# A two-layer graph network on one core: attention of the second layer moved from a stage of its own into the edge loop before it

## The chip, the core and the metric

The kernel runs on one core of a Trainium2 chip. The core has five engines with instruction streams of their own: TensorE (PE; its weight loads are shown apart, as PEld), VectorE (DVE), ScalarE (ACT), GpSimd (POOL) and SyncE (SP), and 16 DMA engines between the memory outside (DRAM here) and the core's own. Each engine takes its instructions in program order and waits at an instruction for what it needs; a transfer is issued by SP, ACT or POOL and then runs by itself. The metric is the device time of one execution in microseconds.

## The reference: what is computed

There are 12500 nodes with 256 features and 200000 directed edges (`src`, `dst`), sorted by `dst`. In short:

```python
h = relu(layernorm(x))
h = h @ W_pre + b_pre
for W, b in ((W1, b1), (W2, b2)):            # two graph convolutions
    z = h @ W
    h = relu(segment_sum(z[src] * norm, dst) + b)   # a self loop at each node as well
x = x + h @ W_post + b_post
h = relu(layernorm(x))
xt = (h @ weight).reshape(n, 4, 64)          # attention
alpha = softmax(leaky_relu((xt[src] * attn_l).sum(-1) + (xt[dst] * attn_r).sum(-1)), over the 4 heads)
out = x + (sum over heads of alpha[i] * xt[dst[i]], repeated 4 times)   # i < 12500: node i uses edge i
```

`norm` is 1/sqrt(degree of source) times 1/sqrt(degree of target). What matters later is the last step: row i of the output uses edge number i, so only the first 12500 edges take part. Edges are sorted by target, so the targets of these edges lie in the first nodes, while their sources lie anywhere.

## The kernel before

**Tiles.** Nodes are cut into 98 tiles of 128 (called windows, `w`). Edges are cut into 112 chunks of 14 tiles of 128 edges (`J = 14`, `CE = 1792`); the last chunk has 9. The 1792 edges of a chunk have targets within 128 nodes of the chunk's first one, so that the whole chunk is summed in one accumulator.

**Preparation.** Up to about 130 us the kernel loads x and the edges, counts the degrees and writes the normed rows to a table in DRAM.

**The edge loop** is `convolve` (from L1185), used twice: pass 1 (first convolution) and pass 2 (second). For each tile of 128 edges:
- POOL gathers 128 source rows from a table in DRAM into the buffer `fgot` (L1397, an indirect DMA). A row of the tables `parts1` and `parts2` is three bf16 parts whose sum is the fp32 row, 1.5 KB in pass 2.
- VectorE has made the chunk's one-hots `fhot` (L1243) in one instruction for all 14 tiles: for each edge a row of 128 zeros and a one at its target's place.
- TensorE adds one-hot times gathered rows to the accumulator `facc`, once for each of the three parts (L1407).

When a chunk is done, `close` copies the accumulator out (`fsums`, ScalarE), turns it (`fturn`, TensorE) and adds it into a sliding buffer of turned sums (`buf`, VectorE, at an offset read from a register). When the buffer's first 128 nodes are complete, `finish` lets a window through: in pass 1 the product with the first layer's folded weights, the split into parts and the write to `parts2`; in pass 2 (`finish2`) two products (`fpz`, `fpo`), the new x (kept in DRAM as `kept_x`), a layer norm, a turn (`fpt`) and the product with the attention weights (`fpx`, L1597).

**The order of work** is written out by hand: each step of a window is put on a list with a due tile (`at`), and after each tile's instructions the loop emits the steps that are due (`run`). The last windows, behind the last tile, run their steps one after the other.

**Buffers.** In pass 2 the gathers have four buffers of 9 tiles, so POOL can be up to 36 tiles ahead of TensorE. A buffer is free again when all its products are done.

**Attention** is a stage of its own behind pass 2 (L1640 to L1792), except for small preparations in pass 2 (`set_up`; target rows of the first chunk). Window by window `fpx` gives the products with the weights and their left and right scores; the left scores of all nodes go to the tables `table_l` and `table_e` in DRAM, the first nine windows' rows to `table_r`. The stage then handles 14 groups of 7 tiles: target rows by products with one-hots (`fends`, L1741), left scores by 98 gathers of 16 bytes a row (`fal`, L1751; those of the last three windows by products, `lacks`, for the first 14 tiles), then a softmax over four heads and the weighted sum on VectorE (`near`, `far`, `some`, `more`, `fmix`), and the output rows (`fres`).

Behind all that stands `general_path`, which runs only where a test of the edges fails (`bad_row`); here it doesn't run.

Of the kernel before, what the change touches and what calls it, by code (L numbers as in the profile page):

```python
# [10 lines left out]
I32 = mybir.dt.int32  # L11
# [402 lines left out]
def fast_path(  # L414
# [51 lines left out]
    complete = [min(max((M * c - LAG) // P, 0), NT) for c in range(NCH)] + [NT]  # L466
    assert NCH <= P and complete[NCH - 1] >= NT - 2
# [11 lines left out]
    assert AC * J == NT and AC * CE <= E and XW < NT  # L479
    table_r = dram.tile([XW * P, DR], F32, name="table_r")  # L480
    table_l = dram.tile([NT * P, H], F32, name="table_l")

    LW = 3
    table_e = dram.tile([NT * P, H], F32, name="table_e")
# [18 lines left out]
    base_b = const.tile([P, NCH], F32, name="base_b")  # L503
    row_i = const.tile([P, AC], I32, name="row_i")
# [88 lines left out]
    with tc.tile_pool(name="fprep", bufs=1) as prep:  # L593
# [233 lines left out]
        with tc.tile_pool(name="fpsum", bufs=2, space=PSUM) as psum, \  # L827
# [227 lines left out]
            wide = prep.tile([NCH, P], F32, name="wide")  # L1055
            nc.vector.tensor_copy(wide, base.to_broadcast([NCH, P]))
# [7 lines left out]
            nc.tensor.matmul(fk[:, 2, :NCH], wide, ident[:NCH, :NCH], start=True, stop=True)  # L1064
# [7 lines left out]
            for f in after:  # L1072
                f()
            after = [raw_block(ends, m, psum.tile([P, 4 * P], F32, name="ft"), j0)
                     for j0 in (8, 12)]
            nc.vector.tensor_copy(base_b, fk[:, 2, :NCH])
            nc.vector.tensor_scalar(row_i, base_b[:, :AC], lane, float(XW * P - 1), op0=ALU.add,
                                    op1=ALU.min)
# [16 lines left out]
    def check_chunks(work, psum):  # L1095

        last = E - (NCH - 1) * CE
        far = work.tile([P, 2, NCH], F32, name="far2", bufs=1)
        nc.vector.tensor_reduce(far[:, 0, :], to_t, AX.X, ALU.min)
        c, (n, r) = NCH - 1, divmod(last, P)  # L1100
        nc.vector.tensor_reduce(far[:, 1, :c], to_t[:, :c, :], AX.X, ALU.max)
        nc.vector.tensor_reduce(far[:, 1, c:], to_t[:, c, None, :n], AX.X, ALU.max)
        if r:
            nc.vector.tensor_tensor(far[:r, 1, c:], far[:r, 1, c:], to_t[:r, c, n:n + 1], ALU.max)
        pt = psum.tile([P, KC + 2, P], F32, name="fpt", bufs=1)
        for i in range(2):
            nc.tensor.transpose(pt[:NCH, i, :], far[:, i, :], ident)
        ends = work.tile([NCH, 2], F32, name="far_ends", bufs=1)
        nc.vector.tensor_reduce(ends[:, 0:1], pt[:NCH, 0, :], AX.X, ALU.min)
        nc.vector.tensor_reduce(ends[:, 1:2], pt[:NCH, 1, :], AX.X, ALU.max)  # L1110
        nc.vector.tensor_scalar(ends[:, 0:1], ends[:, 0:1], 0.0, None, op0=ALU.is_ge)
        nc.vector.tensor_tensor(ends[:, 1:2], ends[:, 1:2], keeps[:, 1:2], ALU.is_lt)
        nc.vector.tensor_mul(ends[:, 0:1], ends[:, 0:1], ends[:, 1:2])
        nc.vector.tensor_mul(ends[:, 0:1], ends[:, 0:1], keeps[:, 0:1])
        nc.tensor.transpose(pt[:1, 2, :NCH], ends[:, 0:1], ident[:NCH, :NCH])
        kept = work.tile([1, 1], F32, name="n_kept", bufs=1)
        nc.vector.tensor_reduce(kept, pt[:1, 2, :NCH], AX.X, ALU.add)
        nc.vector.tensor_add(kept, kept, counted)
        nc.vector.tensor_scalar(bad_row, kept, -1.0, float(NCH + 1), op0=ALU.mult, op1=ALU.add)
# [12 lines left out]
    def load_late(pool):  # L1132

        nc.scalar.dma_start(roots, root_t)
        for t, w in ((wb, w2), (wo, w_post), (wg[:, :, :D], w_gat)):
            nc.scalar.dma_start(t, w.rearrange("(k p) n -> p k n", p=P))
        nc.scalar.dma_start(b2c, b2.rearrange("(k p) -> p k", p=P))
        nc.scalar.dma_start(bob, b_post.partition_broadcast(P))
        attn = []
        for a in (attn_r, attn_l):  # L1140
            ar = pool.tile([P, D], F32, name="far", bufs=2)
            nc.scalar.dma_start(ar, a.rearrange("h c -> (h c)").partition_broadcast(P))
            attn.append(ar)
        return attn

    def late_weights(pool, attn):

        for i, ar in enumerate(attn):
            for k in range(KC):
                prod = pool.tile([P, H, C], F32, name="fprod", bufs=1)  # L1150
                nc.vector.tensor_mul(prod.rearrange("p h c -> p (h c)"), wg[:, k, :D], ar)
                nc.vector.tensor_reduce(wg[:, k, D + i * H:D + (i + 1) * H], prod, AX.X,
                                        ALU.add)

    def convolve(ep, table, stride, width, ahead, with_sum, psum, prepare, finish, parts, since,
                 lacking=False, raw=(), rows_p=None, behind=None):
# [28 lines left out]
        def run(now=None):  # L1185

            while due:
# [3 lines left out]
                do(d)  # L1191

# [41 lines left out]
        const_p = psum.tile([P, P if with_sum else P + D], F32, name="iota_p", bufs=1)  # L1234
        iota_p = const_p[:, :P]
        nc.vector.tensor_copy(iota_p, iota_w)
        if not with_sum:
            state["bias"] = const_p[:, P:]
            nc.vector.tensor_copy(state["bias"], bob)

# [13 lines left out]

        def hot_of(c):

            n = nj[c]
            h = new_hot(c)
            one_hots(h[:, :n, :], to_0 if lacking and c == 0 else to_t[:, c, :n])
            return h  # L1260

        def new_rows_of():
            if with_sum:
                return new_got()
            return rows_p.tile([P, ONE, 3 * stride], BF16, name="fgot", bufs=ahead)

        def late_sums():
# [3 lines left out]
            froms = new_rows_of().rearrange("p j d -> p (j d)")[:, :J * D]  # L1271
            froms = froms.rearrange("p (j d) -> p j d", d=D)
            assert stride == TW * P and D == TW * P
            for i in range(TW):
                one_hots(froms[:, :, i * P:(i + 1) * P], from_0[:, i, :])
            px = psum.tile([P, KC, P], F32, name="fpt", bufs=1)
# [100 lines left out]
        for t, (c, j) in enumerate(tiles):  # L1377
# [4 lines left out]
            if many == 1:  # L1382
                if j == 0:
                    gots = (raw + [spare])[c] if raw and c <= len(raw) else new_rows_of()
                got = gots[:, j, :]
            else:
                i = (t - since * J) % ONE
                if i == 0:
                    gots = new_rows_of()
                    if since:  # L1390
                        gots = gots.rearrange("p j d -> p (j d)").bitcast(BF16)
                        gots = gots[:, :ONE * 3 * stride].rearrange("p (j d) -> p j d", j=ONE)
                got = gots[:, i, :]
# [10 lines left out]
            if j == (5 if some else 2) and c + 1 < NCH:  # L1404
                hots[c + 1] = hot_of(c + 1)
            for i in range(many):
                nc.tensor.matmul(acc, hots[c][:, j, :], got[:, i * stride:i * stride + width],  # L1407
# [10 lines left out]
            if behind:  # L1418
                behind(t)
            run(t)  # L1420
        run()
# [51 lines left out]
    def split_rows(pool, psum):  # L1473
        rows = {}

        def load(w):
            rows[w] = pool.tile([P, D1], F32, name="frow", bufs=4)
            nc.sync.dma_start(rows[w], table1[w * P:(w + 1) * P, :])

        def step(t):  # L1480
# [3 lines left out]
            if k < NT:  # L1484
                load(k)
            if k >= 2:
                p = psum.tile([P, 4, P], F32, name="fpt", bufs=1)
                p = p.rearrange("p a b -> p (a b)")[:, :D1]
                b = pool.tile([P, 3, D1], BF16, name="frow_p", bufs=3)
# [3 lines left out]
                to_parts(p, b, parts1, k - 2)  # L1493

# [5 lines left out]
    assert 3 * D1 * ONE <= 2 * D1 * J and J * D <= 3 * D * ONE  # L1500

    with tc.tile_pool(name="psum1", bufs=1, space=PSUM) as psum, \
# [5 lines left out]
                 lambda w, b, s, pre, _: finish1(work, psum, w, b, s, pre), parts1, SINCE,  # L1508
                 raw=raw, rows_p=late, behind=split_rows(late, psum))
    ring.close()  # L1510

    ap = ctx.enter_context(tc.tile_pool(name="fatt", bufs=2))
    rows = [ap.tile([P, DR], F32, name="rows", bufs=AC) for c in range(AC)]
    EARLY = 2

    FROM = 40
    assert J % G == 0 and FROM > XW + 2 and FROM + J < NT - LW
    lates = {w: ap.tile([P, DA], F32, name="fxl", bufs=LW) for w in range(NT - LW, NT)}
    early = [ap.tile([P, G, DR], F32, name="fxe", bufs=J // G) for g in range(J // G)]
    hot_l = [ap.tile([P, CE], F32, name="hot_l", bufs=LW) for i in range(LW)]  # L1520

    def prepare2(work, w):
# [6 lines left out]
        nc.sync.dma_start(xb[:n, :], x[w * P:w * P + n, :])  # L1531
        return rb, xb

    def finish2(work, psum, w, buf, pre, bias):
        v = {"root": pre[0], "x": pre[1]}

        def d():
            pz = in_psum(psum, w, "fpz", [P, D], "facc", [P, D], 2)
# [16 lines left out]
        def f():  # L1555
            po = v["po"] = in_psum(psum, w, "fpo", [P, D], "facc", [P, D], 2)
# [4 lines left out]
        def g():  # L1561
# [9 lines left out]
            nc.scalar.activation(v["sc"], mv[:, 1:2], AF.Sqrt, bias=eps)  # L1571

# [8 lines left out]
        def i():  # L1581
            pt = v["pt2"] = in_psum(psum, w, "fpt", [P, KC, P], "fturn", [P, 2 * KC, P])
            for k in range(KC):
                nc.tensor.transpose(pt[:, k, :], v["h"][:, k * P:(k + 1) * P], ident)  # L1584

        def k():
            v["ht"] = work.tile([P, KC, P], F32, name="ht2")
            nc.scalar.activation(v["ht"], v["pt2"][:, :KC, :], AF.Copy)  # L1588
# [4 lines left out]
        def q():  # L1593
            px = in_psum(psum, w, "fpx", [P, DA], "iota_p", [P, P + D])
            px = v["px"] = px[:, d0:] if w + 1 < NT else px[:, :H]
# [4 lines left out]
        def r():  # L1600
            if w < NT - LW:
                xa = work.tile([P, DA], F32, name="fxa")
            else:
                xa = lates[w]
            nc.scalar.activation(xa[:, d0:], v["px"], AF.Copy)
            nc.scalar.dma_start(table_l[w * P:(w + 1) * P, :], xa[:, DR:])
            if w < NT - LW:
                nc.scalar.dma_start(table_e[w * P:(w + 1) * P, :], xa[:, DR:])
# [233 lines left out]
```

## Time and profile before

| what | us |
|---|---|
| median of 10 runs (4148.69 to 4157.59) | 4150.46 |
| the profiled execution | 4150.89 |
| its span, first to last instruction | 4149.1 |
| first gather of pass 1 / of pass 2 (start) | 133.9 / 2029.6 |
| last gather of pass 2 (end) | 3987.2 |
| first gather of the attention stage (start) | 4004.1 |
| POOL busy / TensorE / VectorE / ScalarE | 3107.2 / 2794.0 / 1386.7 / 620.4 |
| mean granted TensorE clock | 0.73 |

How to read the views: a *group* line gives a line of the kernel, the engine, the operation, output and inputs, shapes and count; then busy time in us and the mean of one instruction in ns; then the engine's idle time just before these instructions and what ended it. "Issue" is a gap in which the engine waited for nothing that the profile shows. Products overlap, so a group's busy time over its count is what one costs in a row of them, and less than the mean of one. A *window* line gives, for a stretch of time, the busy time of PE, PEld, DVE, ACT and POOL (with instructions), then the granted TensorE clock (1.00 is full), the mean busy share of the DMA engines and GB/s. The *chain* follows the work that ended last back to its causes; printed in order of time it gives start, length and what.

### The profile page before, as it was taken

The numbers are of one execution on the slowest core, as the hardware profiler recorded it, in microseconds if no ns is written. First come the engines' busy times: TensorE is split into PE (matmuls) and PEld (weight loads), VectorE is DVE, ScalarE is ACT, GpSimd is POOL, SyncE is SP. The second block draws the span as 40 slices with busy tenths as digits, with TensorE's granted clock in tenths as the row PEclk, the third lists the DMA queues.
The fourth block names the chain that finished last, engine by engine and source line by source line (L and its number), as shares of the span: only waits on it lengthen the run. The fifth ranks groups of instructions, "written<-read, shape, count | busy, mean of one in ns | idle before, by whom it ended". The sixth has DMA issues, their size and how long they took to land. (4 is left out here: it accounts for less than half of the span.)

```text
span 4149.1 us, 38956 instructions
## 1 busy us (share of the span) xinstructions
PE 2794.0 (67%) x13306; PEld 1909.3 (46%) x13306; DVE 1386.7 (33%) x3009; ACT 620.4 (15%) x1625; POOL 3107.2 (75%) x3299
## 2 busy tenths in 40 slices
PE   7687776767777766777666666666666666666674
PEld 5465444444444444444444444444454444444452
DVE  7677532222222222222322222222222222222238
ACT  5433210100010001001001111111111111111122
POOL 7677777777777777777777777777777777777766
PEclk7697876666666666666678877777777777777777
DMA  8688766666666666666667766776676666666766
GB/s 269 191 247 239 219 176 183 187 183 183 183 185 181 182 186 184 181 183 187 185 182 203 186 180 179 180 185 178 180 180 186 180 180 181 181 180 180 185 195 196
DMA packets 413533, 787.28 MB, mean 190 GB/s; under 512 B 101005, under 2 KB 267172, under 8 KB 413324
## 3 DMA queue, kind: packets, MB, share of 16 engines
q0 software_dynamic: 197264, 594.53, 54.3%
q1 hardware_dynamic: 170214, 173.89, 13.1%
q10 hardware_dynamic: 45846, 16.27, 1.6%
q8 instruction: 107, 1.75, 0.2%
q14 instruction: 102, 0.84, 0.1%
HBM read 692.31 MB, written 92.05 MB: 189 GB/s over the span
## 5 line engine op out<-in xcount | busy, mean ns | idle before, releaser
L1397 POOL DMA_INDIRECT fgot<-parts,fsrc_t x2720 | 2574.4, 946 | 828.6 <-issue 797.2
L1407 PE MATMUL facc<-fgot,fhot 128*128 128x256 bf16 (+2 forms) x8986 | 1943.5, 357 | 1162.6 <-DMA fgot<-parts,fsrc_t 1078.6
L1407 PEld LDWEIGHTS <-fhot 128*128 128x128 bf16 x8202 | 982.0, 121 | 1741.5 <-issue 1475.9
L1243 DVE TENSOR_TENSOR fhot<-iota_p,to_t 128x1792 bf16<-128x1792 f32 (+1 forms) x224 | 449.1, 2005 | 0.0
L1397 POOL DMA_INDIRECT fgot<-ftable,fsrc_t x336 | 318.5, 948 | 115.0 <-issue 103.3
L1468 DVE TENSOR_TENSOR fpo<-fpo,fparts 128x256 f32<-128x256 f32 x97 | 41.8, 431 | 921.5 <-ACT fo L1454 921.5
L1549 DVE SCALAR_TENSOR_TENSOR fy<-rb,fb2c,fpz 128x128 f32<-128x128 f32 x194 | 58.8, 345 | 681.5 <-PE fpz L1542 681.5
L1305 DVE TENSOR_TENSOR buf<-buf,fturn 128x256 f32 x224 | 94.5, 422 | 414.0 <-PE fturn L1208 368.4
L1407 PEld LDWEIGHTS facc<-fgot,fhot 128*128 128x128 f32 x784 | 164.7, 227 | 128.3 <-DMA fgot<-ftable,fsrc_t 79.3
L1563 DVE SCALAR_TENSOR_TENSOR fx<-fpo,fdinv,fxb 128x256 f32<-128x256 f32 x97 | 46.9, 484 | 525.1 <-PE fpo L1558 525.1
L1288 ACT ACTIVATE fsums<-facc 128x257 f32<-128x257 f32 (+1 forms) x224 | 85.4, 381 | 883.4 <-PE facc L1407 877.8
L1445 PE MATMUL fpo<-wf,buf 128*128 128x256 f32 x388 | 164.3, 571 | 25.3 <-DVE buf L1305 25.3
L1542 PE MATMUL fpz<-buf,fwb 128*128 128x128 f32 x776 | 170.8, 395 | 1.4 <-DVE buf L1305 1.4
L1542 PEld LDWEIGHTS fpz<-buf,fwb 128*128 128x128 f32 x776 | 165.0, 313 | 7.7 <-DVE buf L1305 2.0
L1450 ACT ACTIVATE fpo<-fpo,fdinv 128x256 f32<-128x256 f32 x97 | 43.1, 445 | 584.1 <-PE fpo L1446 584.1
L1445 PEld LDWEIGHTS fpo<-wf,buf 128*128 128x128 f32 x388 | 106.4, 299 | 49.3 <-DVE buf L1305 29.5
L1208 PE MATMUL fturn<-fident,self 128*128 128x128 f32 x396 | 97.2, 336 | 26.9 <-DMA self<-ftable 25.2
L1208 PE MATMUL fturn<-fident,fsums 128*128 128x128 f32 x448 | 108.9, 334 | 1.9 <-ACT frow_p L1492 1.5
L1558 PE MATMUL fpo<-fwo,fz 128*128 128x256 f32 x388 | 107.4, 402 | 0.8 <-ACT fz L1552 0.8
L1588 ACT ACTIVATE ht<-fpt 128x256 f32<-128x256 f32 x97 | 37.1, 383 | 441.3 <-PE fpt L1584 440.4
L1751 POOL DMA_INDIRECT fal<-table_l,fsrc_t x84 | 81.2, 967 | 25.6 <-issue 23.2
L1552 ACT ACTIVATE fz<-fy 128x256 f32<-128x256 f32 x98 | 40.8, 417 | 392.7 <-DVE fy L1549 344.6
(284 smaller groups left out, 2411.1 us busy)
## 6 DMA issues: line engine op xcount, KB each, us to landing
fgot<-parts,fsrc_t POOLq DMA_INDIRECT x2720
parts<-frow_p SPq DMA_DIRECT2D x98, 195.0 KB
parts<-fparts SPq DMA_DIRECT2D x98, 192.0 KB
frow<-ftable SPq DMA_DIRECT2D x98, 130.0 KB
self<-ftable SPq DMA_DIRECT2D x99, 128.0 KB
self<-ftable SPq DMA_DIRECT2D x97, 130.0 KB
ftable<-fo ACTq DMA_DIRECT2D x98, 128.0 KB
kept_x<-fx SPq DMA_DIRECT2D x98, 128.0 KB
```

The source lines that it names most:

```text
L1208: nc.tensor.transpose(v["pt"][:, i * KC + k, :], rows[:, k * P:(k + 1) * P], ident)
L1243: nc.vector.tensor_tensor(h, iota_p[:, None, :].to_broadcast([P, n, P]), to[:, :, None].to_broadcast([P, n, P]), ALU.is_equal)
L1288: nc.scalar.activation(sb, acc, AF.Copy)
L1305: nc.vector.tensor_add(b, b, v["pt"][:, :KC, :])
L1397: nc.gpsimd.indirect_dma_start(out=got, out_offset=None, in_=rows_of[:(NT - TW) * P, :] if some else rows_of[:], in_offset=bass.IndirectOf ...
L1407: nc.tensor.matmul(acc, hots[c][:, j, :], got[:, i * stride:i * stride + width], start=(j == 0 and i == 0), stop=(j == nj[c] - 1 and i == ...
L1445: nc.tensor.matmul(po, buf[:, k, :P], wf[:, k, :], start=(k == 0), stop=False)
L1542: nc.tensor.matmul(pz[:, m, :], wb[:, k, m * P:(m + 1) * P], buf[:, k, :P], start=(k == 0), stop=(k == KC - 1))
L1549: nc.vector.scalar_tensor_tensor(y[:, m, :], v["root"], b2c[:, m:m + 1], v["pz"][:, m, :], op0=ALU.mult, op1=ALU.add)
L1558: nc.tensor.matmul(po, v["z"][:, m, :], wo[:, m, :], start=(m == 0), stop=(m == KC - 1))
L1563: nc.vector.scalar_tensor_tensor(x2, v["po"], dinv[:, w:w + 1], v["x"], op0=ALU.mult, op1=ALU.add)
L1751: nc.gpsimd.indirect_dma_start(out=al[:, i, :], out_offset=None, in_=(table_l if c else table_e)[:], in_offset=bass.IndirectOffsetOnAxis(a ...
```

## The change

Attention goes into pass 2, and its stage is replaced by a short one for the "late" edges.

1. **Narrower one-hots.** `PARTS` tells which of the 128 places the edges of a tile can have: tiles 1 to 5 of a chunk the first 64, 6 to 9 the first 96, 10 to 12 the last 64; the first and the last tile keep all 128. VectorE makes them in five instructions, and the product adds to `acc[lo:hi, :]` alone. It holds in pass 2 and in pass 1 from the chunk where bf16 parts begin. `check_chunks` tests these ranges. The rows stay as three bf16 parts.
2. **Buffers.** Three buffers of 14 tiles in place of four of 9 in pass 2; they are placed at another address. In pass 1 the fp32 rows to be split are loaded a step later, into a ring of two.
3. **A list of the late edges** (`list_late`, in pass 1): of the first 12500 edges those whose source lies in the last 14 windows (`LATE = 84`) are counted, numbered and put in 16 lists of 128, with source, target and place. It also writes the sources' and targets' low parts as bf16 rows to DRAM (`lo_rows`, `rel_rows`).
4. **Attention in pass 2** (`attend`). Left scores stay on the core (`l_all`), and the writes of `table_l` and `table_e` go. Work items are queued and put behind tiles by `feed`, each with a number of tiles to the next one:

```python
for t in range(0, NT, G):        # after window 9: rows of the targets, one load a tile
    items.append((when("w", XW), G, [lambda t=t + i: ends_of_tile(t) for i in range(G)]))
for b in range(NG):              # right scores
    items.append((when("w", XW), 4, alpha_r(b)))
...                              # one-hots and target rows of the late lists, to DRAM
for s in range(len(STAGES) - 1): # left scores by products, for windows 0-17, 18-35, 36-53, 54-71
    for b in range(NG):
        items.append((when("w", STAGES[s][1]), 4, alpha_l(s, b)))
for b in range(NG):              # after window 84: windows 72-83, softmax, mix, output
    items.append((when("w", LATE), 8, group(b)))
```

   `NG` is 14 and `G` is 7 tiles. `alpha_l` loads the low parts of the sources to all partitions, makes a one-hot of 128 x 896 in fp32 on VectorE, multiplies it with the left scores of 18 (or 12) windows (72 or 48 columns) and keeps, by a mask and a sum, those of the right window:

```python
def product():
    v["p"] = bank()[:, :G * nw * H].rearrange("p (t w h) -> p t w h", t=G, h=H)
    for j in range(G):
        nc.tensor.matmul(v["p"][:, j, :, :], v["h"][:, j * P:(j + 1) * P],
                         l_all[:, w0:w1, :], start=True, stop=True)
```

   A `group` does that for the fifth stage and goes on, in 15 steps of a tile each: softmax, a turn, 7 products that spread the shares (`pick`, 128 columns), weights on VectorE, 7 products with the target rows (64 columns), then the sum with the kept x and the store of 7 tiles of the output. The kept rows have two buffers. All these products are fp32. The rows of late edges are stored too, with their scores incomplete.
5. **The end** (`tail_begins` and the block behind `convolve`): the lists' one-hots and target rows are loaded, the kept x rows gathered (`fetch_x`, 11 and then 5 gathers), and once the last window's scores are there, 16 products, masks, a softmax and sums for the 16 lists; the rows are scattered over those in the output:

```python
for i in range(k0, k0 + n):
    nc.gpsimd.indirect_dma_start(
        out=out[:], out_offset=bass.IndirectOffsetOnAxis(ap=late_i[:, 0, i:i + 1], axis=0),
        in_=sets["x"][:, i, :], in_offset=None)
```

The core of the diff for the edge loop:

```diff
+    PARTS = [(0, 6, 0, P // 2), (6, 10, 0, P - P // 4), (10, J, P // 2, P)]
...
-            return rows_p.tile([P, ONE, 3 * stride], BF16, name="fgot", bufs=ahead)
+            return rows_p.tile([P, J, 3 * stride], BF16, name="fgot", bufs=ahead)
...
+            hot, lo, hi = part(c, j) if many > 1 else (hots[c][:, j, :], 0, P)
             for i in range(many):
-                nc.tensor.matmul(acc, hots[c][:, j, :], got[:, i * stride:i * stride + width],
+                nc.tensor.matmul(acc[lo:hi, :], hot,
+                                 got[:, i * stride:i * stride + width],
...
-            if behind:
-                behind(t)
+            if every:
+                every(t)
+            feed(t)
             run(t)
-        run()
+        if at_end:
+            at_end()
+        while due or behind:
+            t += 1
+            feed(t)
+            run(t)
```

## The prediction

> **What bounds the kernel now.** I read the busy shares of the page first, then its costliest groups, then the windows, and the chain last. The first fence is from the page: busy time by engine, then two groups (busy time, mean of one, idle time before it and what ended it).
>
> ```profile
> PE 2794.0 (67%) x13306; PEld 1909.3 (46%) x13306; DVE 1386.7 (33%) x3009; ACT 620.4 (15%) x1625; POOL 3107.2 (75%) x3299
> ...
> L1397 POOL DMA_INDIRECT fgot<-parts,fsrc_t x2720 | 2574.4, 946 | 828.6 <-issue 797.2
> L1407 PE MATMUL facc<-fgot,fhot 128*128 128x256 bf16 (+2 forms) x8986 | 1943.5, 357 | 1162.6 <-DMA fgot<-parts,fsrc_t 1078.6
> ```
>
> A gather takes POOL 946 ns, and 0.30 us of "issue" follows (797.2 us over 2720 of them): nothing that the profile shows delays the next one, so POOL is full at one gather per 1.25 us though it reads 75%. TensorE waits for gathers (1078.6 us) and for little else. Windows (each engine's busy time, clock, DMA share, GB/s) of pass 2, of three stretches of 10 us, and of the stage behind the last tile:
>
> ```profile
> 2100.00:3900.00 1800.00, 1157.72 (x6330) 858.72 (x6330) 480.64 (x1018) 220.81 (x586) 1362.02 (x1438) 0.77 0.70 183
> 3950.00:3960.00 10.00, 9.03 (x42) 6.79 (x41) 1.33 (x4) 0.42 (x1) 7.57 (x8) 0.54 0.66 163
> 3960.00:3970.00 10.00, 6.64 (x50) 5.11 (x47) 6.92 (x22) 2.61 (x7) 7.56 (x8) 1.00 0.72 207
> 4010.00:4020.00 10.00, 5.23 (x37) 4.37 (x36) 2.14 (x6) 0.93 (x3) 7.56 (x9) 0.69 1.05 347
> 4004.00:4149.00 145.00, 73.97 (x252) 47.66 (x251) 108.21 (x202) 34.62 (x100) 95.13 (x98) 0.71 0.68 211
> ```
>
> In pass 2 POOL issues 1438 gathers in 1800 us, while TensorE is 64% busy, VectorE 27%, ScalarE 12%, and the DMA share is 0.70. The last row is what the change attacks: 145 us after the last window (4004) in which attention runs alone, led by its own 98 gathers. The chain of waits, in order of time, shows them (start, length):
>
> ```profile
> 4010.31 1.64 POOL fal L1751
> 4012.26 6.08 DMA fal<-table_e,fsrc_t
> 4020.36 4.26 PE fends L1741 x10
> 4024.62 6.08 PE lacks L1722 x42
> ...
> 4086.14 3.10 DMA fal<-table_l,fsrc_t
> ...
> 4095.37 2.32 DMA fal<-table_l,fsrc_t
> ```
>
> **The sum, part by part.** It is made against the profiled execution: last gather done 3987.2, last window through 4004, span 4149.1, time 4150.9 (1.8 around the span; 0.4 above the median of the ten runs).
>
> *Removed:* the stage from 4004 to 4149, 145 us on the path.
>
> *Gathers of the two passes:* as many as before, of the same bytes. POOL's pace of 1.25 us stays the floor; the last gather can't end before about 3987. The depth in front of TensorE goes from 36 to 42 tiles. Change in POOL's own work up to there: one gather fewer, nothing.
>
> *Narrower one-hots:* five tiles of 14 keep 64 columns at the low side, four 96, three 64 at the high side, two all 128. VectorE builds 1152 columns for 1792: 2.02 us becomes some 1.5 in five instructions, on an engine that is 27% busy: nothing. Weight loads (118 ns for 128 columns) shrink; if they all stood in front of their product, 42 ns a product would go, if none, nothing. TensorE waits for gathers either way: 0 now, up to 1 us per 8 tiles where it becomes late (below).
>
> *Pass 1:* the late edges are listed there (14 batches of some 2 us on VectorE, small bf16 products), the bound checks get longer, rows are fetched one step later with two buffers. All of it lies under POOL's gathers, with VectorE at 25% from 600 to 2000 us; cost nothing, or some 30 us if VectorE were so late that all five gather buffers filled. Dropping the base row from the preparation: under 1 us.
>
> *Attention inside pass 2.* Four stages of 14 batches, each batch in 4 tiles (5 us): 7 fp32 products of 72 columns, one comparison of 896 elements, a masked sum, one broadcast load of 229 KB. An fp32 product is two matmul records; bounds for one, from the groups of before:
>
> ```profile
> L1722 PE MATMUL lacks<-fxl,hot_l 128*128 128x4 f32 x84 | 11.0, 268 | 0.0
> L1542 PE MATMUL fpz<-buf,fwb 128*128 128x128 f32 x720 | 159.1, 396 | 0.0
> L1407 PE MATMUL facc<-fgot,fhot 128*128 128x256 bf16 x4308 | 844.0, 332 | 642.7 <-DMA fgot<-parts,fsrc_t 627.4 <-DVE nb L1576 5.3 <-DVE fhot L1243 3.8
> ```
>
> Busy time over count: 131 ns a record with 4 columns, 221 with 128; a product costs 0.26 to 0.44 us, and I take 0.33. A batch adds 2.3 us of TensorE to 3.2 (64% of 5): 5.5 for 5, behind by 0.5 x 14 = 7 us at the end of a stage, which the 42 tiles (52 us) cover and the 230 tiles between stages give back. VectorE: 1.3 + 1.1 (the `near` row, 896 elements) + about 1.5 for the masked sum = 3.9 of 5. Cost: nothing. SyncE also starts 98 small loads whose address it reads first, one a tile; I find no row for that on SyncE. VectorE's own such read costs 0.35 us (33.4 us of issue before 95 `buf` adds); at up to 2 us each SyncE would fall 74 us behind and hold the windows' loads. I take the near row: nothing.
>
> *The groups are where it is tight.* From the 84th window on (tile 1404 of 1563: its chunk 96 ends at tile 1357, then 13 and 34 steps), 14 groups of 7 tiles run, one in 8 tiles, that is 10 us. Each adds 21 fp32 products (7 of 48 columns, 7 of 128, 7 of 64) = 7 us, between 5.5 and 9.3. TensorE then needs 6.4 + 7 = 13.4 us for 10, less up to 1 for the narrower weights: 13. The DMA engines need 7.0 (share 0.70) plus 2.3 MB (0.92 kept rows in, 0.92 results out, 0.46 broadcasts) at 330 GB/s (347 at share 1.05 in the fence): 14.0 for 10, in 12 of the 14 groups. VectorE: 2.7 + 1.1 + 1.5 + 1.6 (softmax) + 1.2 + 2.0 (`fres` row) = 10.1. So TensorE falls 14 x 3 = 42 us behind, the DMA engines 12 x 4 = 48, side by side, not one after the other. The 42 tiles of depth just hold this, so POOL runs on; 41 tiles (51 us) are left, in which a third of TensorE's time catches up 18 us. **The last tile comes 28 us late** (bounds: 9 with products of 0.26, 62 with 0.44).
>
> *The new tail* after the last window: 32 records for the late scores, 131 to 221 ns each, 5 us; mask and sum over 448 elements, 0.62 each, the first half beside the products, 1.9; softmax with seven short operations of 0.2, an exp of 0.23 with its 1.28 table load, and handovers, 3.4; first two lists' product, sum and add, 0.7 each, 2.1. Then 16 scatters at POOL's 1.25 = 20, and 3 us for the last to land (the chain's shorter landings are 2.3 and 3.1). The rest of VectorE's work (13 us) lies under the scatters. Beside the first 12.4 us, the last kept rows land (3), five gathers fetch them (6.2) and land (3): next in line, level with it. The first 11 of these gathers (13.8 us of POOL) and 3.1 MB of loads (9.4 us at 330 GB/s) lie beside the 17 us of the last windows, where POOL has nothing else. Sum 35.4.
>
> 4004 + 28 + 35.4 = 4067 span; **forecast 4069 us**, 1.9% less.
>
> [...] The granted clock was 0.54 in one stretch and 1.00 in the next, and the bf16 product took 231 ns in the first (26 in 6.0 us) and 161 in the second (46 in 7.4). [...]
>
> **Rivals.**
> 1. *All of it hides:* TensorE does an fp32 product in 0.26 us and the DMA engines take more than 330 GB/s. For it: 353 GB/s occurs in the first 100 us. 4004 + 35.4 + 1.8 = 4041. Chance 0.14.
> 2. *The scatters wait for each other,* since all write the one output tensor: 16 x (1.25 + 2.3) = 57 for 20: 4106. For it: every indirect transfer of before writes to its own tile, so nothing shows the contrary; against: the rows are disjoint. Chance 0.18.
> 3. *Slower: the group's chain sets the period.* Its 15 steps pass between VectorE, TensorE and ScalarE in order: 1.0 + 2.3 + 1.5 + 1.6 + 1.3 (table) + 0.5 + 1.3 + 0.6 + 1.0 + 0.5 + 2.3 + 2.0 = 16 us, with handovers near 20. If two groups can't overlap, because each engine stands at its place in the line, with SyncE held by the two buffers of kept rows, a group takes 20 us instead of 10: 140 late, 18 back, 4004 + 122 + 35.4 + 1.8 = 4163. It decides from 19 us a group (14 x 9.1 - 18 = 110, all that the tail gives). Against it: the steps are spaced so that two groups are in flight. Chance 0.16.
> 4. *The tests of the narrower ranges fail* and the general path runs after all: thousands of us more. The ranges have room for these edges (128 a tile, some 8 nodes): 0.02.
>
> **How the numbers follow.** Forecast (4050 to 4103 by its bounds) 0.46; rivals 0.14, 0.18, 0.16, 0.02; between, near no change, 0.04. Range 4035 to 4125: it takes in the forecast, the first rival and most of the second, and leaves the third out. A measurement of this kernel can tell 0.2% from no change. Faster by more: 0.46 + 0.14 + 0.18 = 0.78; within 0.2%: 0.04; slower: 0.18.
>
> **What would show it.** In the profile after: gathers still 1.25 us apart up to tile 1400, and the last of them before 4000; waits of the products for gathers gone while the groups run, DMA share there near 1; last tile 10 to 60 us after the last gather's old time; some 20 us of scatters. Wrong if POOL waits for TensorE in the stages, if the scatters stand 3 us apart, or if the groups are stretched to 19 us.

## The result, and the profile after

The changed kernel takes 4170.87 us (median of 8 runs, 4161.97 to 4183.43) where the kernel before took 4151.23 beside it: 1.0049 times as long (95% interval 1.0041 to 1.0058). It is slower by half a per cent; 4069 had been forecast, and 4035 to 4125 as the range. The profiled execution took 4169.26 us, its span is 4167.4.

The page, in the same three lines as of before (busy time by engine; gathers; edge products):

```profile
PE 3061.2 (73%) x14819; PEld 2194.4 (53%) x14819; DVE 1534.5 (37%) x4287; ACT 623.8 (15%) x1627; POOL 3031.3 (73%) x3226
...
L1456 POOL DMA_INDIRECT fgot<-parts,fsrc_t x2720 | 2571.7, 945 | 906.4 <-issue 797.6
L1467 PE MATMUL facc<-fgot,fhot 128*64 128x256 bf16 (+6 forms) x8986 | 1891.2, 352 | 737.4 <-DMA fgot<-parts,fsrc_t 715.3
```

The gathers cost what they did (945 ns, 797.6 us of "issue"). But 78 us more stand in front of them (906.4 for 828.6), and TensorE is busy for 267 us more. The windows of the last 300 us say where; first the changed kernel (busy time of PE, PEld, DVE, ACT, POOL, then clock, DMA share, GB/s):

```profile
3800.00:3900.00 100.00, 89.77 (x456) 75.27 (x457) 53.49 (x134) 17.34 (x37) 71.03 (x76) 0.65 0.86 271
3900.00:4000.00 100.00, 90.62 (x433) 74.80 (x433) 50.29 (x120) 17.45 (x36) 39.63 (x43) 0.59 0.73 224
4000.00:4100.00 100.00, 88.49 (x452) 69.50 (x452) 40.88 (x115) 21.78 (x52) 37.30 (x41) 0.72 0.58 176
```

and the kernel before in the first of them:

```profile
3800.00:3900.00 100.00, 64.89 (x360) 48.53 (x359) 26.74 (x57) 11.81 (x32) 75.62 (x80) 0.79 0.68 180
```

Up to 3883 POOL runs at its pace of 80 gathers in 100 us; the four stages of left scores did not disturb it. The groups begin at 3795 and fill TensorE (90% busy, at a granted clock of 0.65 and then 0.59); from 3883 on POOL waits, and falls to half its pace. What POOL waits for from 3800 us on (us in total, times, longest):

```profile
POOL fgot L1456 <- PE facc L1467: 77.7, 6, 19.6
POOL fgot L1456 <- issue: 42.3, 139, 0.3
POOL fgot L2249 <- DMA kept_x<-fx: 28.0, 1, 28.0
POOL out_dram L2293 <- DMA out_dram<-fgot,late_i: 24.8, 13, 2.4
```

The first line is new: the buffers of gathered rows are all full, and POOL waits for TensorE to free one. The products with weights (L2148) run from 3810.9 to 4043.5 in 14 groups: **one group in 17.9 us**. In that stretch TensorE is busy for 211 of 232.5 us:

```profile
3811.00:4043.50 232.50, 211.18 (x1022) 175.38 (x1023) 117.83 (x288) 40.21 (x83) 120.51 (x128) 0.61 0.77 242
```

The last line of the waits belongs to the scatters, seen in the timeline (start, length, what, idle time before):

```profile
4139.07 0.97 POOL L2293 DMA_INDIRECT out_dram<-fgot,late_i  x1 [1.70 <-DMA out_dram<-fgot,late_i]
4141.74 0.97 POOL L2293 DMA_INDIRECT out_dram<-fgot,late_i  x1 [1.70 <-DMA out_dram<-fgot,late_i]
4144.94 0.97 POOL L2293 DMA_INDIRECT out_dram<-fgot,late_i  x1 [2.23 <-DMA out_dram<-fgot,late_i]
```

Each waits until the one before has landed. The account, in spans: the last window's scores are done at 4096.3 (before: 4004), 92 late (70 at the last gather, the rest in tiles that still stand in front of TensorE); the new tail takes 71.1 to 4167.4; the old stage's 145 are gone. 92.3 + 71.1 - 145.1 = +18.3, which is 4167.4 - 4149.1.

### The profile page after: what moved, and what is told of

Read it like the earlier page. It is cut to its first block, busy times and chain, and to the rows that moved or that the text cites. A ratio compares the mean times of both kernels' runs of the same rounds, so it can differ in the third digit from the quotient of the medians.

```text
span 4167.4 us, 43803 instructions
## 1 busy us (share of the span) xinstructions
PE 3061.2 (73%) x14819; PEld 2194.4 (53%) x14819; DVE 1534.5 (37%) x4287; ACT 623.8 (15%) x1627; POOL 3031.3 (73%) x3226
## 5 line engine op out<-in xcount | busy, mean ns | idle before, releaser
L1456 POOL DMA_INDIRECT fgot<-parts,fsrc_t x2720 | 2571.7, 945 | 906.4 <-issue 797.6
L1467 PE MATMUL facc<-fgot,fhot 128*64 128x256 bf16 (+6 forms) x8986 | 1891.2, 352 | 737.4 <-DMA fgot<-parts,fsrc_t 715.3
L1467 PEld LDWEIGHTS <-fhot 128*64 128x64 bf16 (+2 forms) x8202 | 1034.0, 138 | 1267.4 <-issue 1063.6
L1319 DVE TENSOR_TENSOR fhot<-iota_p,to_t 128x128 bf16<-128x128 f32 (+3 forms) x973 | 311.4, 383 | 0.2 <-PE fY L1343 0.2
L1864 DVE SCALAR_TENSOR_TENSOR fy<-rb,fb2c,fX 128x128 f32<-128x128 f32 x194 | 58.7, 344 | 513.6 <-PE fX L1857 513.6
L2076 PE MATMUL behind<-l_all,hot_s 128*128 128x72 f32 (+1 forms) x980 | 159.9, 330 | 77.8 <-DVE hot_s L1975 45.5
L2076 PEld LDWEIGHTS behind<-l_all,hot_s 128*128 128x128 f32 x980 | 153.2, 245 | 88.0 <-issue 59.2
L1857 PE MATMUL fX<-buf,fwb 128*128 128x128 f32 x776 | 179.9, 405 | 1.6 <-DVE buf L1369 1.6
L1857 PEld LDWEIGHTS fX<-buf,fwb 128*128 128x128 f32 x776 | 154.9, 297 | 33.4 <-issue 31.2
L1878 DVE SCALAR_TENSOR_TENSOR fx<-fX,fdinv,fxb 128x256 f32<-128x256 f32 x97 | 46.8, 483 | 293.2 <-PE fX L1873 293.2
L1873 PE MATMUL fX<-fwo,fz 128*128 128x256 f32 x388 | 107.3, 401 | 0.8 <-ACT fz L1867 0.8
```

Source lines behind the costliest of these rows:

```text
L1319: nc.vector.tensor_tensor(v, iota_p[:, None, lo:hi].to_broadcast([P, j1 - j0, hi - lo]), to[:, j0:j1, None].to_broadcast([P, j1 - j0, hi - ...
L1456: nc.gpsimd.indirect_dma_start(out=got, out_offset=None, in_=rows_of[:(NT - TW) * P, :] if some else rows_of[:], in_offset=bass.IndirectOf ...
L1467: nc.tensor.matmul(acc[lo:hi, :], hot, got[:, i * stride:i * stride + width], start=(j == 0 and i == 0), stop=(j == nj[c] - 1 and i == man ...
L1857: nc.tensor.matmul(pz[:, m, :], wb[:, k, m * P:(m + 1) * P], buf[:, k, :P], start=(k == 0), stop=(k == KC - 1))
L1864: nc.vector.scalar_tensor_tensor(y[:, m, :], v["root"], b2c[:, m:m + 1], v["pz"][:, m, :], op0=ALU.mult, op1=ALU.add)
L1873: nc.tensor.matmul(po, v["z"][:, m, :], wo[:, m, :], start=(m == 0), stop=(m == KC - 1))
```

## The experiments

**Theory:** the groups are bound by TensorE, whose work in a group is larger than forecast, and the tail by scatters that wait for each other. **Rivals:** the chain of a group's 15 steps sets its period, or the DMA engines do. A side question is whether the narrower one-hots cost nothing. One remark on numbers: the first six runs were on chips on which the kernel before itself takes 4908 us instead of 4150 (in the first run's trace TensorE stands for 851 us of "issue" in front of the edge products), so their times compare only among themselves; the later runs were on chips that take 4150.

"Period" is the distance of two groups: first to last start of the products with the target rows, over 13 (the last start is that of the last group's last product, which makes every period up to 0.2 us too long). "POOL waits" is from 3800 us on, for `facc`. All columns behind the ratio are from the profiled execution. The profiles differ by up to 10 us in where pass 2 starts (its first gather: 2027.7 to 2037.5), and the last three columns contain that.

| kernel | median us, ratio to before | period | POOL waits | last gather | first, last scatter | span |
|---|---|---|---|---|---|---|
| the change (result) | 4170.9, 1.0049 | 17.9 | 77.7 | 4056.4 | 4110.3, 4154.1 | 4167.4 |
| the change again | 4172.3, 1.0050 | 17.7 | 75.7 | 4061.9 | 4112.6, 4156.5 | 4169.8 |
| one-hots of 128 columns | 4157.5, 1.0010 | 17.3 | 67.4 | 4046.6 | 4093.9, 4137.5 | 4150.9 |
| groups in bf16 | 4122.3, 0.9922 | 14.4 | 24.7 | 4010.5 | 4061.4, 4105.2 | 4118.5 |
| both, 14 scatters | 4116.8, 0.9916 | 14.5 | 26.8 | 4010.1 | 4058.8, 4095.9 | 4108.9 |
| and a load ahead | 4105.4, 0.9878 | 13.1 | 12.9 | 4005.0 | 4055.0, 4092.1 | 4105.0 |
| two groups only | 4082.9, 0.9836 | | none | 3984.7 | 4021.2, 4064.8 | 4078.2 |

**One-hots of 128 columns everywhere (first on a slower chip).**

```diff
-    PARTS = [(0, 6, 0, P // 2), (6, 10, 0, P - P // 4), (10, J, P // 2, P)]
+    PARTS = [(0, 6, 0, P), (6, 10, 0, P), (10, J, 0, P)]
```

> The change with one-hots of 128 columns everywhere, all else as changed. Theory (TensorE is the bound while the groups run, and weight loads of 64 and 96 columns take 141 and 178 ns where those of 128 take 120): the edge products get cheaper, groups come closer than 17.9 us by about half a us, the whole is 5 to 12 us shorter than the changed kernel (about 4160 us), and TensorE's busy share in pass 1 goes from 74% back to 71%. Rival (narrow one-hots cost TensorE nothing or help it): 0 to 5 us longer than the changed kernel.

Measured: 5164.6 us, 1.052 of before (1.047 to 1.056); period 21.3. From 3000 to 4000 us TensorE is busy for 578 us with 3196 records, and for 632 with 3179 in the next run, which has the narrow one-hots. There is no time of the change itself on that chip, so only the last point tells something: narrow loads mean more TensorE time, not less.

**The scatters to 16 tensors of their own** instead of the output.

```diff
-                    out=out[:], out_offset=bass.IndirectOffsetOnAxis(ap=late_i[:, 0, i:i + 1],
+                    out=aside[i][:], out_offset=bass.IndirectOffsetOnAxis(ap=late_i[:, 0, i:i + 1],
```

> The change with each of the 16 scatters writing to a DRAM tensor of its own instead of the output (late rows of the output are left incomplete). Theory (each scatter waits for the one before to land, since all write one tensor): scatters 1.25 us apart instead of 2.9, VectorE's sums next in line, 22 to 26 us off, about 4146 us. Rival (the spacing is what POOL needs to write rows to DRAM): unchanged at 2.9 us, 4171 us.

Measured: 5150.4 us, 1.048 (1.043 to 1.054). The timeline of this kernel:

```profile
5123.78 0.98 POOL L2294 DMA_INDIRECT aside<-fgot,late_i  x1 [0.31 <-issue]
5125.06 0.97 POOL L2294 DMA_INDIRECT aside<-fgot,late_i  x1 [0.30 <-issue]
5126.34 0.97 POOL L2294 DMA_INDIRECT aside<-fgot,late_i  x1 [0.30 <-issue]
```

1.28 us apart, with nothing before them but "issue"; the 16 take 5122.5 to 5142.2, 19.7 us, where those into one tensor took 43.7 on the same chip. The 24 us in between are the waits, and what makes them is the shared target, not the engine.

**The groups' products in bf16.**

```diff
-    pick = ap.tile([G * H, G, P], F32, name="pick")
+    pick = ap.tile([G * H, G, P], BF16, name="pick")
...                                  # likewise hot_s, turned_a, weights; copies of l_all and ends
+                v["e"] = ap.tile([P, G, C], BF16, name="ends_b", bufs=2)
+                nc.scalar.activation(v["e"], ends[:, t, :C], AF.Copy)
```

> The change with the three sets of products of a group in bf16 (scores, shares and target rows rounded to bf16 there): the same steps and hand-overs, one matmul record instead of two for each product. Theory (TensorE is the bound while the groups run): a group goes from 17.9 us to about 12, where the DMA engines (13.9 by the estimate) or VectorE may take over; 55 to 85 us off, 4085 to 4115 us. Rival (the chain of steps between engines sets the period): a group stays above 16 us, at most 20 us off, 4150 us or more.

Measured: 5121.5 us, 1.045 (1.040 to 1.050), period 18.0. Beside the wide one-hots' 5164.6 that is 43 us less; but two things differ between those two, so the run alone doesn't settle it.

**No kept rows in, no results out** in the 12 whole groups.

```diff
-                    v["kept"] = load_kept(b * G, G)
...
-                    add_mix(b * G, G, v["kept"], v["p"])
```

> The change without the loads of kept x rows, the sum and the stores of the output in the 12 whole groups (left out, so most of the output isn't written): 22 MB of transfers less while the groups run. Theory (TensorE is the bound): groups still 17 to 18 us apart, total within 6 us of the changed kernel. Rival (the DMA engines are the bound while the groups run): groups 10 to 13 us apart, 50 to 80 us off.

Measured: 5167.9 us in one run, period 20.5, beside 22.0 in the run with the scatters apart, which has these transfers. The DMA share in the stretch 4760 to 5030 falls from 0.60 to 0.41, the period by 1.5. The DMA engines are not what a group waits for there. VectorE's sum of these groups is left out as well, so the 1.5 us are not the transfers' alone.

**Two repeats on another slower chip.**

> The kernel of the third run (the groups' products in bf16) once more, in the hope of a chip on which the kernel before takes its 4150 us. Theory (TensorE is the bound while the groups run): groups about 12 us apart instead of 17.9, 4085 to 4115 us. Rival (the chain of steps sets the period): groups above 16 us, 4150 us or more.

> The kernel of the first run (one-hots of 128 columns everywhere) once more, for the same reason. Theory (narrow weight loads cost TensorE more than full ones): 5 to 12 us less than the changed kernel, about 4160 us. Rival (narrow one-hots are free or help): 0 to 5 us more.

Measured: 5122.9 (1.0445, 1.0423 to 1.0467) with period 18.0, and 5158.5 (1.052, 1.050 to 1.054) with 21.1: both as in their first runs.

**The change itself again.**

> The changed kernel itself, unaltered, as the base for the other runs of this study (the chips of the six runs so far take about 4908 us for the kernel before, against 4150 in the result). If the kernel before takes about 4908 us here too: with the narrow one-hots TensorE is the bound nearly everywhere on such a chip, so by the theory that narrow weight loads are slower it takes 10 to 60 us more than the run with full one-hots (5158 to 5165), that is 5170 to 5220; by the rival that narrower loads are cheaper or cost nothing it is 5150 to 5165 or below. If the kernel before takes about 4150 us: 4162 to 4183, as in the result.

Measured: 4172.3 us, 1.0050 (1.0033 to 1.0067), beside 4151.7 of before: the second case. It is the base for the rest.

**Full one-hots, bf16 groups and 14 scatters.** The edits above and

```diff
-            for i in range(k0, k0 + n):
+            for i in range(k0, min(k0 + n, KL - 2)):
```

> Three edits of the changed kernel at once: one-hots of 128 columns everywhere, the groups' products in bf16, and 14 scatters instead of 16 (the last two lists hold no late edge with these inputs, so the output is whole; more than 1792 late edges would be lost). Theory (TensorE bounds the groups, the scatters land one after the other): the gains add up. Against the changed kernel on the same chip: 43 us for bf16 (5165 to 5122 in the runs so far), 5.6 us for two scatters of 2.8, and what full one-hots give; where the kernel before takes 4908 us that is 5105 to 5120, a ratio of 1.040 to 1.043. Where the kernel before takes 4150 us: the groups at 12 to 14 us instead of 17.9 give 13 x 4 to 6 = 50 to 75 us, the scatters 5.6, the one-hots 0 to 10: 4085 to 4115, faster than the kernel before by 1 to 1.5 per cent. Rival (the chain of steps of a group sets its period): bf16 and full one-hots change little, 4155 to 4170.

Measured: 4116.8 us, 0.9916 (0.9900 to 0.9933): faster than the kernel before. The period falls to 14.5 and TensorE is busy for 62.13 us in 3900 to 4000 instead of 90.62. That is 2 us over what was expected, 4085 to 4115: something else is late now (below, a load ahead). The output is whole only because the last two lists hold no edge with these inputs.

**Two groups instead of 14.**

```diff
-        for b in range(NG):
+        for b in range(NG - 2, NG):
             items.append((when("w", LATE), 8, group(b)))
```

> Leaves out 12 of the 14 groups of the attention (the first 84 tiles of the output are not written; only the two groups whose sums the last windows use are left), all else as in the changed kernel. Both theories of the groups: the loop ends as if there were no groups. Where the kernel before takes 4150 us: last gather at about 3990 to 4005, end at 4070 to 4095 (the new tail of 71 us and some of the last windows' 39), so the groups cost 75 to 100 us together. Where the kernel before takes 4908 us: the groups were 21.3 us apart there, of which a part is the loop's own pace, so 100 to 180 us less than the changed kernel. If it gains less than 50 us, the lateness does not come from the groups but from the steps ahead of them or from the narrow one-hots.

Measured: 4082.9 us, 0.9836 (0.9820 to 0.9853). The window of 3900 to 4000 and the gathers after 2999 us (durations least, median, most; first and last start):

```profile
3900.00:4000.00 100.00, 72.60 (x364) 52.13 (x363) 30.85 (x92) 14.57 (x41) 75.79 (x79) 0.76 0.70 208
```

```profile
L1456 POOL DMA_INDIRECT fgot<-parts,fsrc_t x788: 942/946/2496, 2999.4 to 3984.7; - x197
```

POOL stays at its pace and the last gather ends where it did before the change (3986; 3987). All of the lateness of the edge loop comes from 12 groups: 4172.3 - 4082.9 = 89 us; the page's 78 us of waits are what POOL saw of it. The stages before them, the pass-1 list and the buffers add nothing.

**The groups in bf16 alone, on a chip that takes 4153 us for the kernel before.**

> The changed kernel with the groups' products in bf16 and nothing else; on chips where the kernel before takes 4908 us the edit took the changed kernel with full one-hots from 5158 to 5165 down to 5121 (those runs had different one-hots). Theory (TensorE bounds the groups): three times 14 fp32 records of 0.21 us become 21 of about 0.24, so TensorE's share of a group falls by 4 us or more, and the period from 17.8 to the 14 to 15 that the chain allows: 13 x 3 to 4 = 39 to 52 us, 4120 to 4135, a ratio of 0.992 to 0.996. Rival (the chain was the bound all along): 4160 to 4175.

Measured: 4122.3 us, 0.9922 (0.9907 to 0.9937): 50 us less than the change. Its group products, and what TensorE waits for in front of them (from 3780 us on):

```profile
L2141 PE MATMUL behind<-turned_a,pick 28*128 28x128 bf16 x98 | 12.4, 254 | 1.6 <-ACT turned_a L2135 1.3
L2156 PE MATMUL behind<-ends_b,weights 128*128 128x64 bf16 x98 | 7.7, 238 | 3.8 <-DVE weights L2148 3.8
L2082 PE MATMUL behind<-l_b,hot_s 128*128 128x48 bf16 x98 | 5.9, 205 | 36.6 <-DVE hot_s L1978 36.6
```

Half as many records, 26 us in all where the change has 121 (42.8, 39.0 and 39.0), and POOL's waits for `facc` are 24.7 for 77.7. The stretch of the groups:

```profile
3811.60:3998.20 186.60, 123.49 (x750) 86.75 (x749) 117.35 (x291) 45.51 (x96) 124.48 (x131) 0.67 0.92 298
```

TensorE's busy time falls from 16.2 to 9.5 us a group, and the period of 17.9 by 3.5. These products are steps of the chain too, and the edit shortens both, so this run by itself does not part TensorE from the chain. The trace of the change does: there TensorE is busy for 16.2 of the 17.9 us and waits for steps of the chain in only 1.6. So TensorE is what binds the groups of the change. At 14.4 the next bound stands, seen in the last line: the products wait for `hot_s`, the first link of the chain.

**One-hots of 128 columns alone, on the same chip.**

> The changed kernel with one-hots of 128 columns in all edge tiles and nothing else. Theory: weight loads of 64 and 96 columns are slower than those of 128, and that costs where TensorE is the bound: 24 edge products of a group at 14 ns less each and their loads, 0.3 to 1 us a group, so 4 to 13 us over the groups: 4158 to 4168, a ratio of 1.0015 to 1.004; outside of the groups TensorE's busy share falls by 3 to 4 points and nothing moves, because POOL sets the pace there. Rival (narrow one-hots cost nothing, or help as VectorE makes them faster): 4170 to 4176, or above.

Measured: 4157.5 us, 1.0010 (1.0001 to 1.0019), against 1.0050 of the change (on another chip, so by the ratios to the kernel before): the narrow one-hots cost 0.4%, some 16 us; 4 to 13 had been expected. The weight loads in pass 1 (1000 to 1900 us) of the change, then of this kernel (busy time, mean ns):

```profile
L1467 PEld LDWEIGHTS <-fhot 128*64 128x64 bf16 x1236 | 165.8, 141 | 320.6 <-issue 301.7
L1467 PEld LDWEIGHTS <-fhot 128*96 128x96 bf16 x612 | 102.5, 178 | 48.7 <-issue 41.2
...
L1467 PEld LDWEIGHTS <-fhot 128*128 128x128 bf16 x309 | 35.6, 120 | 50.9 <-issue 42.1
```

```profile
L1467 PEld LDWEIGHTS <-fhot 128*128 128x128 bf16 x2156 | 269.3, 127 | 463.5 <-issue 380.1
```

64 columns (141 ns) take longer to load than 128 (120 in the first of the two, 127 in the second), and 96 (178) longer still. It costs nothing where POOL sets the pace (in the two profiles pass 2 starts at 2027.9 and 2027.7, and from 3000 us on each has 786 gathers) and time where TensorE does. The kernel of three edits, where TensorE no longer binds, fits with that: its 4116.8 is less than the 4122.3 of bf16 alone by about what two scatters of 2.9 us cost, which leaves nothing for the wide one-hots. The intervals of these two overlap, so this is a hint.

**A load ahead:** that kernel, with the row of a group's sources loaded one group earlier into a second buffer.

```diff
-                v["row"] = row_of(lo_rows, b, "lo_all", 1)
+                if short:
+                    v["row"] = ahead.pop(b, None) or row_of(lo_rows, b, "lo_all", 2)
...
+                if b + 1 < NG:
+                    ahead[b + 1] = row_of(lo_rows, b + 1, "lo_all", 2)
```

> The kernel with full one-hots, bf16 products in the groups and 14 scatters (4116.8 us beside 4151.7 of the kernel before), and one edit more: the row of a group's sources (lo_all) has two buffers instead of one and is loaded by the group before, so that a group no longer starts with a load. In that kernel the groups were 14.5 us apart, TensorE was busy for 62 per cent of their stretch, and what it waited for was hot_s, which waited for lo_all (39.2 us for 12 groups, 7.5 us from issue to use). Theory: with TensorE relieved the chain of a group's steps is the bound, and its first link is this load: the period falls by 2 to 4 us to 10.5 to 12.5, 13 x 2 to 4 = 26 to 50 us, and the end comes 20 to 36 us earlier (the loop can't gain more than the 36 us by which it is behind the kernel with two groups): 4080 to 4097. Rival (the DMA engines, busy at 0.88 to 0.95 in that stretch, set the pace): the load ahead changes nothing, 4110 to 4120.

Measured: 4105.4 us, 0.9878 (0.9863 to 0.9893), the fastest version that writes all rows. The gain is smaller than expected: 1.4 us of the period (14.5 to 13.1), 4 us between the two profiled spans, 11 between the medians (the later profile starts pass 2 at 2037.5, the earlier at 2030.6, which is the difference). TensorE's wait for `hot_s` fell from 39.3 to 20.6 us; the window shows what is near its limit in its place:

```profile
3900.00:4000.00 100.00, 68.01 (x470) 50.74 (x469) 67.94 (x163) 28.57 (x60) 66.98 (x70) 0.70 0.92 308
```

The DMA share is 0.92 (0.95 from the first to the last group). Both stories hold a part: the load was the first link of the chain, and behind it stand the DMA engines. Which share of the remaining 3 us over POOL's 10 each has was not separated.

## Why the prediction was wrong

**Right:** the gathers' pace as the floor; the four stages, the list in pass 1, the buffers and SyncE's reads free (the run with two groups ends its gathers at 3986; the 2 us for such a read, set against 0.35, were an assumption); the narrower one-hots free in the passes, where TensorE waits; VectorE and the DMA engines in a group: 10.1 and 14.0 us were forecast, 9.1 (117.83 / 13) and 13.8 (0.77 x 17.9) measured.

**The step that failed first: "TensorE then needs 6.4 + 7 = 13.4 us for 10, less up to 1 for the narrower weights: 13."** From 3811 to 4043.5, 13 groups of the change:

```profile
L2148 PE MATMUL behind<-ends_all,weights 128*128 128x64 f32 x195 | 42.5, 408 | 0.0
L1467 PE MATMUL facc<-fgot,fhot 128*64 128x256 bf16 x174 | 39.7, 382 | 0.0
L2133 PE MATMUL behind<-turned_a,pick 28*128 28x128 f32 x182 | 36.2, 351 | 0.1
L2076 PE MATMUL behind<-l_all,hot_s 128*128 128x48 f32 x168 | 33.7, 378 | 14.2 <-DVE hot_s L1975 9.2 <-DVE sc L1890 4.9
L1467 PE MATMUL facc<-fgot,fhot 128*96 128x256 bf16 x96 | 24.2, 382 | 0.0
```

Busy time over count gives 218, 199 and 201 ns for a record of the group, so 0.40 to 0.44 us for an fp32 product, not 0.33: it is the upper end of the bounds, even with 48 columns. With the turn (4.6 us), which the 7 left out, that is 117 us, 9.0 a group for 7. The edge products take 228 and 252 ns, 234 on the mean with the wide tiles: 5.6 us a group. Before the change those behind 3811 us took 195 (81.8 / 420):

```profile
L1407 PE MATMUL facc<-fgot,fhot 128*128 128x256 bf16 x420 | 81.8, 328 | 58.6 <-DMA fgot<-parts,fsrc_t 58.2
```

The windows' products are another 3 (rows overlap a little, so they add up to more than the sum). TensorE is busy for 211 of 232.5 us, 16.2 a group for 13, and idle for 1.6, mostly where the chain hands over.

Where the two sizes went wrong: 0.33 was the middle between rows with 4 and with 128 columns, and all three widths here cost like 128. Both sizes also came from stretches in which TensorE has pauses, at a clock of 0.77 to 0.79; in the groups it is full, at 0.61. For the fp32 products the kernel with two groups points to the clock: in the window that holds its groups (3800 to 3900) the clock is 0.76 with TensorE 79% busy, and they cost 0.35 to 0.36 us. But no run varied the clock by itself, so this is not shown. Of the edge products' 39 ns over 195, the narrow weights make more than half: from 3780 to 4100 us they take 219 ns (107.5 us over 491), and 194 with one-hots of 128 columns (95.6 over 492). So "up to 1" gained by narrower weights has the wrong sign: they cost 16 us in all. The 42 ns a product behind it, 118 in proportion to the columns, were my estimate; no run shows loads of 64 or 96 columns getting shorter.

**The next step went with it: "The 42 tiles of depth just hold this, so POOL runs on."** It would have held for the 3 us a group of the forecast; it did not for 7.9. POOL first waits at 3883 and ends 70 us late. 13 x (17.9 - 10) = 103 us were lost, the last window comes 92 late; the forecast was 42 to 48 lost and 28 late, and its upper bound of 62 was still too low.

**The second step that failed: "16 scatters at POOL's 1.25 = 20, and 3 us for the last to land."** The first 12.4 us of the tail were 14.0. But first to last scatter start takes 43.8, as in the second rival (57 for all 16 with the last landing; they take 46), whose condition was met: one output tensor. From the last scatter's start to the end of the span another 13.3 pass, of which 2.4 are its landing; in every kernel with this tail the span ends 13 us after that start (what fills the rest, no row shows), and I had counted 3; before the change it ended 8.2 us after the start of the last store (4140.9), which the forecast left out. So the tail is 71.1 for 35.4. In this program the scatters into the output wait for each other though their rows are disjoint: 13 waits of 1.7 to 2.4 us (24.8 in all) end with the landing before them, and they are gone with 16 tensors.

**The third rival** had the right outcome, 17.9 us a group with its bound at 19, by another mechanism: not the chain but TensorE. The chain was there behind it: in bf16, at 14.4, TensorE waits for its first link. What it gave as the break-even also moved, since the tail was dearer: with a tail of 71, 145 - 71 = 74 us of lateness are enough.

The sum: 92 - 28 = 64 us from the groups and 71 - 35 = 36 from the tail make the 100 between the forecast span, 4067, and 4167.4.

## What to carry to other kernels

When work is to be hidden under an engine that waits a third of its time, price it at what the engine does when it is full, not at its mean over a stretch with pauses, and ask how long the excess lasts against the depth of the buffers. An fp32 product was two records at 48, 64 and 128 columns alike (196 for 98 products of each); here the same products in bf16 turned a loss of 0.5% into a gain of 0.8%. And look at the target of each write: scatters into one tensor stood in line, 2.9 us each, where those into tensors of their own went out every 1.28.

## What the runs showed of the hardware

**The narrower one-hots loaded more slowly.** 141 ns for 64 columns, 178 for 96, 120 to 127 for 128, bf16. From 64 to 96 the time grows, and at 128 it is below both. The traces show the times, not what makes them.

**The fullest stretch had a low clock, but the clock did not follow the load.** In pass 2 it was 0.79 at 65% busy (before, 3800 to 3900), 0.76 at 73 to 79% (two groups), 0.59 at 91% (the change). Out of that order, pass 1 of the kernel before had 0.66 at 71% (1000 to 1900), and the bf16 groups 0.67 to 0.69 at 67% with the DMA engines at 0.87 to 0.95, then 0.91 at 81% right after. With TensorE idle (4120 to 4160 of the change) it was 0.50. What sets it stays open; no run varied it by itself.

**Scatters into one tensor waited for each other in this program,** 2.7 to 3.4 us from start to start, with a landing of 2.4 us for 128 rows of 1 KB.
